# Experts on sorted slots of token-expert pairs with gathered weights, and mixed heads by the turning product

## The chip, the cores and the metric

The kernel runs on one core of a Trainium2 chip, all in f32. The metric is device time in microseconds of one execution. The engines are TensorE (PE; its weight loads are listed apart as PEld), VectorE (DVE), ScalarE (ACT), GpSimd (POOL) and SyncE (SP, which issues the DMAs). Each engine executes its own instructions in order; they wait for each other by semaphores.

## The reference

A pre-norm decoder of four layers, twelve sublayers in a row, each `x = x + f(layernorm(x))` on x of 8 x 256 x 256. Two of them are touched. Sublayer 3 is a mixture of 8 experts with 2 chosen for each token, and one shared expert that all tokens pass through (256 wide, 512 hidden):

```python
router_probs = softmax(flat @ router_w + router_b)          # flat: 2048 x 256
topk_probs, topk_idx = top_k(router_probs, 2)
weights = zeros_like(router_probs).at[arange(T)[:, None], topk_idx].add(topk_probs)
shared_out = gelu(flat @ sw1 + sb1) @ sw2 + sb2
h1 = gelu(einsum('td,edh->teh', flat, rw1) + rb1[None])
expert_out = einsum('teh,ehd->ted', h1, rw2) + rb2[None]
return shared_out + einsum('ted,te->td', expert_out, weights)
```

Sublayer 4 is attention with 16 heads of 16, whose scores are mixed over the heads before the softmax and whose probabilities are mixed over the heads behind it (q and k are turned by rope):

```python
dots = einsum('bhid,bhjd->bhij', q, k) * 16 ** -0.5
attn = softmax(einsum('bhij,gh->bgij', dots, w_pre))
attn = einsum('bhij,gh->bgij', attn, w_post)
out = einsum('bhij,bhjd->bhid', attn, v)
return out.transpose(0, 2, 1, 3).reshape(B, T, E) @ w_out.T + b_out
```

## The kernel before

x stays in SBUF for the whole kernel, as four blocks of 512 tokens (two sequences each), a block being four tiles of 128 tokens. Two threads of the program, left (blocks 0 and 1) and right (blocks 2 and 3), each go through the twelve layers: ssm, perceiver16, moe, talking, biased, routed, windowed, perceiver4, signs, recurrent, crossed, ternary. Each layer is a generator that yields after a small piece of work. `build` interleaves the two by a virtual time: the table `SHARE` says how long a layer is to last, `steps_of` how many pieces it has, and the right thread starts 1.01 x `SHARE[ssm]` later and runs so much faster that both end together. A scheduler in the framework then fixes each engine's order of instructions and the semaphores. So while one thread is in one layer, the other's work of an earlier or later layer fills the engines.

All of `Net`'s helpers are shared by both threads. `mms` (L361) issues the matmuls of a sum, so most matmuls have that line; `together` (L369) issues column-group matmuls, whose stationary operand is 32 or 64 columns wide, next to each other; `copy` takes PSUM to SBUF, two times of three on ACT (L353) and else on DVE (L355); `norm` computes a layer norm, its power on POOL (L382); `turned` transposes normed rows (L394); `add_rows` adds a bias to x on POOL (L421); `add_product` and `project` multiply by an output matrix and add to x on DVE (L428); `top2` ranks the router's probabilities by comparing each with each on DVE (L452 to L458).

`moe` (L760 on): per block a norm, its transpose `xt`, the router, softmax and `top2`; then a loop over the shared expert (-1) and the eight experts, each on all 512 tokens of each block: 4 x 2 matmuls of 512 columns (`mm<-xt,we`) with a gelu after each pair on ACT (L806), then for each of four tiles 4 matmuls of 256 columns (`o<-we,h`), whose result times the token's weight is added to x on DVE (L822). The weight is zero where the expert was not chosen. An expert's weights (1 MB) come by two DMAs of 512 KB on SP's queue (L795), two buffers of them.

`talking` (L846 on): per block a norm, q and k by `roped`, v; then for each sequence 16 steps, one for each output head h. A step scales q by column h of `w_pre` on DVE (`qs`, L875), so that the 256-wide product with k is already the mixed score; two tiles of 128 query tokens make 4 matmuls of 256 columns (`sc<-k,qs`), then a maximum (DVE L885), the exponential with its sum (ACT L889), the division (DVE L897, L899), four transposes (`pt`, L912), a copy (`pv`), and 4 matmuls of 256 columns against values that POOL has scaled by `w_post` for this head (`vh`, L903), summed in PSUM over all 16 steps (`o<-pv,vh`, L920).

The other layers that the prediction names: ssm (first; its rows reach SBUF by way of DRAM, the products on POOL are L593), perceiver16, `biased` and `routed` after `talking`, and a column-of-ones product in `ternary` (L1813).

Of the kernel before, what the change touches and what calls it, by code (L numbers as in the profile page):

```python
# [8 lines left out]
F32 = mybir.dt.float32  # L9
U8 = mybir.dt.uint8  # L10
AF = mybir.ActivationFunctionType
# [62 lines left out]
def constants():  # L74
# [21 lines left out]
    k.add("sums", (p[:, None] == 32 * np.arange(4)[None, :] + 16).astype(f))  # L96
    k.add("half", (p[:, None] // 64 == p[None, :] // 64).astype(f))
    for n in (8, 4):
        e = np.arange(n)
        k.add(f"before{n}", np.broadcast_to((e[None, :] < e[:, None]).astype(f).reshape(1, -1), (128, n * n)))  # L100
# [27 lines left out]
def layout(a):  # L128
# [37 lines left out]
    for k in ("ln_m_g", "ln_m_b", "ln_l_g", "ln_l_b"):  # L166
# [8 lines left out]
    p.add("rb1", a[n + "rb1"].reshape(8, 4, 128).transpose(2, 0, 1))  # L175
# [6 lines left out]
            a[n + "rw2"].reshape(8, 4, 128, 256).transpose(0, 2, 1, 3).reshape(8, 128, 1024),  # L182
        ],
        2,
    )
# [6 lines left out]
    p.mat("pre", np.repeat(a[n + "w_pre"].T, 16, axis=0))  # L192
    put("w3", p)
    rows("r3", ("post", a[n + "w_post"].T), ("bo", a[n + "b_out"]))
# [101 lines left out]
class Net:  # L296
# [145 lines left out]
    def top2(self, p, n, m, of=None):  # L442


        nc = self.nc
        rank = self.small.tile([128, n, m], F32, name="rank", tag=f"rank{m}")
        for i in range(n):
# [8 lines left out]
            nc.vector.tensor_reduce(rank[:, i, :], gt, AX.X, ALU.add)  # L456
        w = self.small.tile([128, n, m], F32, name="top", tag=f"top{m}")
        nc.vector.scalar_tensor_tensor(w, rank, 1.5, p if of is None else of, ALU.is_lt, ALU.mult)  # L458
# [43 lines left out]
def ssm(net):  # L502
# [3 lines left out]
    with net.scope(mm=2, y=1):  # L506
# [9 lines left out]
        for blk in net.blks:  # L516
# [19 lines left out]
            for d in "fb":  # L536
# [6 lines left out]
                nc.sync.dma_start(rows[d], dbc[d][64:96])  # L543
            yield
# [215 lines left out]
def moe(net):  # L760

    nc = net.nc
    with net.scope(mm=2, o=2):
        es = net.work
        w, r = net.weights(2)
        xts, tops = [], []
        for blk in net.blks:
            xt = net.normed_turned(blk, bufs=len(net.blks))
# [7 lines left out]
            p = net.small.tile([128, 4, 8], F32, name="probs", tag="probs")  # L776
# [7 lines left out]
            top = es.tile([128, 4, 8], F32, name=f"topall{blk}")  # L784
            nc.vector.tensor_copy(top, net.top2(p, 4, 8))
            tops.append(top)
            net.add_rows(blk, r["sb2"])
            yield
        for e in range(-1, 8):
            if e < 0:  # L790
                w1, w2, b1 = w["sw1"], w["sw2"], w["sb1"]
            else:
                we = es.tile([128, 2048], F32, name="we", bufs=2)
                for j in range(2):
                    nc.sync.dma_start(  # L795
                        we[:, j * 1024 : j * 1024 + 1024], net.d["experts"][e][:, j * 1024 : j * 1024 + 1024]
                    )
                w1 = we[:, :1024].rearrange("p (k m) -> p k m", k=2)
                w2 = we[:, 1024:].rearrange("p (k m) -> p k m", k=4)
                b1 = w["rb1"][:, e, :]  # L800
            for blk, xt, top in zip(net.blks, xts, tops):
                h = es.tile([128, 4, 512], F32, name="h", bufs=2)
                for c in range(4):
                    ps = net.bank()
                    net.mms(ps, [(w1[:, kc, c * 128 : c * 128 + 128], xt[:, kc, :]) for kc in range(2)])
                    nc.scalar.activation(h[:, c, :], ps, AF.Gelu, bias=b1[:, c : c + 1])  # L806
                    yield
                for i in range(4):
                    pairs = [(h[:, c, i * 128 : i * 128 + 128], w2[:, c, :]) for c in range(4)]
                    o = net.bank("o")  # L810
# [33 lines left out]


def talking(net):  # L846

    nc = net.nc
    with net.scope(mm=1, sc=1, pt=1, o=1):
        work = net.work  # L850
# [1057 lines left out]
```

## Time and profile before

| what | us |
|---|---|
| median of three runs (5421.10, 5433.18, 5438.67) | 5433.18 |
| profiled execution | 5411.81 |
| its span, first to last instruction | 5410.0 |
| mean granted TensorE clock in it | 0.91 |

In the profile, "x1024" behind a group counts instructions; the numbers behind the bar are busy time in us and mean ns of one; then the engine's idle time ahead of them and what ended it. An f32 matmul is two records of PE. PE's ends are modelled. The groups of the two layers, in numbers: the experts' first products 236.9 us and second ones 241.3 us of PE; the mixed heads' scores 293.6, transposes 94.1 and value products 265.0 us; the eight experts' DVE additions 61.8, `qs` 86.1, the maxima 88.1, ex times rc 99.6 us of DVE, `vh` 156.2 us of POOL. The left thread is in moe from about 1590 to 1950 us of the span and in talking until 2830; the right one in moe from 2450 to 2840 and in talking until 3510.

The DMA traffic of the whole span is 160 MB at a mean of 30 GB/s; all DMAs of before go out by SP.

### The profile page before, as it was taken

The numbers are of one execution on the slowest core, as the hardware profiler recorded it, in microseconds if no ns is written. First come the engines' busy times: TensorE is split into PE (matmuls) and PEld (weight loads), VectorE is DVE, ScalarE is ACT, GpSimd is POOL, SyncE is SP. The second block draws the span as 40 slices with busy tenths as digits, with TensorE's granted clock in tenths as the row PEclk, the third lists the DMA queues.
The fourth block names the chain that finished last, engine by engine and source line by source line (L and its number), as shares of the span: only waits on it lengthen the run. The fifth ranks groups of instructions, "written<-read, shape, count | busy, mean of one in ns | idle before, by whom it ended". The sixth has DMA issues, their size and how long they took to land.

```text
span 5410.0 us, 55906 instructions
## 1 busy us (share of the span) xinstructions
PE 4599.5 (85%) x20488; PEld 2846.3 (53%) x20488; DVE 2992.7 (55%) x5672; ACT 1981.2 (37%) x4524; POOL 1442.2 (27%) x1223
## 2 busy tenths in 40 slices
PE   5566567787889999999998899888898999988979
PEld 2121123343446556656766666655555677755656
DVE  6778788678781344442346554566556464243352
ACT  3444445445541433332432222323334332333221
POOL 3546534325340011110123422234121100232122
PEclk8888889898989999999999899986778999988989
DMA  3111121111110100001010000000001000010000
GB/s 97 48 47 55 50 82 49 32 31 45 41 60 24 57 14 1 1 7 36 24 35 1 34 1 1 29 13 34 12 1 41 8 6 32 1 51 35 2 32 16
DMA packets 95477, 160.15 MB, mean 30 GB/s; under 512 B 6651, under 2 KB 82275, under 8 KB 90851
## 3 DMA queue, kind: packets, MB, share of 16 engines
q1 hardware_dynamic: 95203, 156.58, 9.2%
q8 instruction: 162, 2.65, 0.2%
q14 instruction: 112, 0.92, 0.1%
HBM read 152.67 MB, written 3.88 MB: 29 GB/s over the span
## 4 chain that ended last, share of the span: by engine, by line
PE 51%; DVE 11%; ACT 4%; issue 3%; POOL 3%; POOLq 0%; ACTq 0%; DVEq 0%
PE mm L361 25%; PE o L361 6%; PE sc L369 5%; PE o L920 4%; PE sc L361 4%; PE av L369 3%; PE pt L912 1%; PE mm L705 1%; DVE xn L384 1%; ACT ex L889 1%; PE mm L394 1%; PE mm L1736 1%; DVE nm L885 1%; DVE ex L899 1%; DVE pv L355 1%
## 5 line engine op out<-in xcount | busy, mean ns | idle before, releaser
L609 PE MATMUL y<-hc,consts 128*128 128x512 f32 x1024 | 637.4, 724 | 334.7 <-DVE hc L603 333.3
L593 POOL TENSOR_TENSOR db<-du,rep 128x512 f32<-128x512 f32 x512 | 645.6, 1269 | 407.8 <-DVE mm L599 306.4
L599 DVE TENSOR_TENSOR_SCAN mm<-mm,db 128x512 f32<-128x512 f32 x512 | 619.0, 1220 | 62.3 <-ACT mm L585 62.0
L609 PEld LDWEIGHTS y<-hc,consts 128*128 128x128 f32 x1024 | 181.6, 211 | 669.7 <-DVE hc L603 630.8
L903 POOL TENSOR_TENSOR vh<-v,w 128x256 f32<-128x256 f32 x256 | 156.2, 631 | 955.2 <-PE o L920 927.3
L361 PE MATMUL mm<-xt,w 128*128 128x512 f32 (+1 forms) x896 | 359.5, 532 | 26.4 <-DVE rope_s L842 8.3
L603 DVE TENSOR_TENSOR hc<-mm,rep 128x512 f32<-128x512 f32 x512 | 348.2, 686 | 32.5 <-PE y L609 3.2
L585 ACT ACTIVATE mm<-dl,nega_b 128x256 f32<-128x256 f32 x512 | 241.0, 476 | 210.4 <-DVE hc L603 197.9
L585 ACT ACTIVATE mm<-dl,nega_f 128x256 f32<-128x256 f32 x512 | 239.9, 476 | 199.2 <-DVE hc L603 185.7
L361 PE MATMUL sc<-k,qs 128*128 128x256 f32 x1024 | 293.6, 404 | 22.2 <-ACT ex L889 21.3
L369 PE MATMUL sc<-k,q 64*128 64x333 f32 (+1 forms) x1152 | 260.1, 508 | 56.4 <-ACT pex L695 32.7
L353 ACT COPY pv<-mm 111x384 f32<-111x384 f32 (+2 forms) x334 | 172.5, 517 | 369.4 <-PE mm L705 178.8
L382 POOL TENSOR_TENSOR rs<-ve,neghalf 128x4 f32<-128x4 f32 (+1 forms) x57 | 58.9, 1034 | 887.3 <-DVE ve L380 806.5
L369 PE MATMUL av<-pv,v 111*64 111x256 f32 (+5 forms) x2752 | 254.0, 381 | 18.8 <-DVE pv L355 10.9
L920 PE MATMUL o<-pv,vh 128*128 128x256 f32 x1024 | 265.0, 395 | 5.2 <-ACT pv L353 3.5
L361 PE MATMUL mm<-h,sw 128*128 128x256 f32 x1024 | 242.5, 382 | 0.0
L361 PE MATMUL o<-we,h 128*128 128x256 f32 x1024 | 241.3, 380 | 1.0 <-DVE x L822 1.0
L361 PEld LDWEIGHTS mm<-xt,w 128*128 128x128 f32 x896 | 165.0, 197 | 146.7 <-issue 79.2
L705 PE MATMUL mm<-consts,pex 128*111 128x128 f32 x960 | 187.9, 308 | 63.5 <-DVE pex L701 32.9
L705 PEld LDWEIGHTS mm<-consts,pex 128*111 128x111 f32 x960 | 144.0, 191 | 185.3 <-DVE pex L701 52.0
L361 PE MATMUL mm<-xt,we 128*128 128x512 f32 x512 | 236.9, 594 | 0.3 <-ACT h L806 0.3
L361 PEld LDWEIGHTS sc<-k,qs 128*128 128x128 f32 x1024 | 187.5, 201 | 71.9 <-ACT ex L889 34.8
(372 smaller groups left out, 8512.2 us busy)
## 6 DMA issues: line engine op xcount, KB each, us to landing
we<-in_experts SPq DMA_DIRECT2D x32, 512.0 KB, 4.8
w<-in_w SPq DMA_DIRECT2D x12, 1024.0 KB, 6.9
w<-in_w SPq DMA_DIRECT2D x8, 1025.0 KB, 7.0
rep<-rows0f SPq DMA_DIRECT2D x32, 256.0 KB, 4.7
rep<-rows0b SPq DMA_DIRECT2D x32, 256.0 KB, 4.7
rep<-rows1f SPq DMA_DIRECT2D x32, 256.0 KB, 4.9
rep<-rows1b SPq DMA_DIRECT2D x32, 256.0 KB, 3.5
rep<-rows2f SPq DMA_DIRECT2D x32, 256.0 KB, 4.9
```

The source lines that it names most:

```text
L353: self.nc.scalar.copy(out, in_)
L361: self.nc.tensor.matmul(out, lhsT=lhs, rhs=rhs, start=n == 0, stop=n == len(pairs) - 1)
L369: self.nc.tensor.matmul(out, lhsT=lhs, rhs=rhs, start=start, stop=stop, tile_position=at)
L382: nc.gpsimd.tensor_tensor(rs[:rows], ve[:rows], self.neghalf[:rows, :n], ALU.pow)
L585: nc.scalar.activation(st[:, m * S : (m + 1) * S], dl[:, 2 * c + m, :], AF.Exp, scale=neg_a[d][:, 2 * c + m, n : n + 1],)
L593: nc.gpsimd.tensor_tensor(pairs_of(db), du[:, 2 * c : 2 * c + 2, :], bc[:, n % 2, 0, :].unsqueeze(1).to_broadcast(both), ALU.mult,)
L599: nc.vector.tensor_tensor_scan(st[:, order], st[:, order], db[:, order], 0.0, ALU.mult, ALU.add)
L603: nc.vector.tensor_tensor(pairs_of(hc), pairs_of(st), bc[:, n % 2, 1, :].unsqueeze(1).to_broadcast(both), ALU.mult,)
L609: nc.tensor.matmul(y[c], lhsT=net.ident, rhs=hc, start=d == "f" and n == 0, stop=d == "b" and n == 15,)
L705: nc.tensor.transpose(pt[:CH, j * 128 : j * 128 + 128], ex[:, e, j * CH : (j + 1) * CH], net.ident)
L903: nc.gpsimd.tensor_tensor(vh[:, j, :].rearrange("p (g e) -> p g e", g=H), v[:, 2 * b + j, :].rearrange("p (g e) -> p g e", g=H), r["post"] ...
L920: nc.tensor.matmul(o[:, c * S : (c + 1) * S], lhsT=vh[:, j, c * 128 : c * 128 + 128], rhs=pv[:, j, :], start=h == 0 and j == 0 and c == 0, ...
```

## The change

**Experts.** The tokens' ranks are kept (`ranks`, split off from `top2`). `places` counts, over the side's 8 tiles, how many pairs of token and chosen expert each expert has (a product with a lower triangle of ones and one with all ones, `ahead` and `ones`), lays the experts out in slots of 128 rows, and gives for each token the row of its two pairs (`rows`), their probabilities (`gate`), and for each slot the rows of its expert's weights in DRAM (`which`). There are 2 x 8 + 7 = 23 slots a side, enough for any choice. Each tile's normed rows are written by two indirect DMAs (POOL's queue) to the table `slots` in DRAM, which was filled with zeros by one DMA on SP in ssm. `read_after` makes the slots' loads wait for all 16 of these writes, and `apart_from_each_other` says that they don't overlap one another. The shared expert runs on all tokens as before. Then each slot: its expert's weights with the bias `rb1` (128 rows of 2052 values) by an indirect DMA on POOL's queue, three buffers; its rows from `slots` by SP; two transposes, a copy, 8 matmuls of 128 columns, 4 gelus, 4 matmuls of 256 columns, a copy, and a store to the table `results` by SP. At the end each token tile gets its two rows by two indirect DMAs from `results` and adds them with their probabilities.

**Mixed heads.** A step no longer is one output head but two groups of 8 tokens with all 16 heads: the stationary operand `qs` holds 16 heads x 8 tokens, made on POOL. Maximum, exponential and sum are the same. Instead of transposing ex, it is multiplied by `mix` (`blend`, which is `w_post` where the token is the same and zero elsewhere, times the reciprocal sums), which transposes and mixes the heads in one product ("turning product"). `pv` of all 16 steps is kept; v is kept in two copies with the odd or the even heads zeroed; at the end of a sequence 32 column-group matmuls make the output. PSUM has two banks for scores, none for `o`.

`SHARE` of moe goes from 270 to 150, and its `steps_of` with it. The diff's core, mostly its new lines (the removed ones are those of `moe` and `talking` above):

```diff
     k.add("sums", (p[:, None] == 32 * np.arange(4)[None, :] + 16).astype(f))
+    k.add("eighth", (p[:, None] % 8 == np.arange(8)[None, :]).astype(f))
     k.add("half", (p[:, None] // 64 == p[None, :] // 64).astype(f))
+    k.add("ahead", (p[:, None] < p[None, :]).astype(f))
+    k.add("row", p[:, None].astype(f))
+    k.add("slots", np.broadcast_to(np.arange(32, dtype=f)[None, :], (128, 32)))
+    k.add("slotrows", np.broadcast_to(np.arange(8, dtype=f)[None, :] * f(128), (128, 8)))
...
-    p.add("rb1", a[n + "rb1"].reshape(8, 4, 128).transpose(2, 0, 1))
...
+            a[n + "rb1"].reshape(8, 4, 128).transpose(0, 2, 1),
         ],
         2,
...
+    ).reshape(8 * 128, 2052)
...
+    p.add("post", np.repeat(a[n + "w_post"].T, 8, axis=0))
     put("w3", p)
-    rows("r3", ("post", a[n + "w_post"].T), ("bo", a[n + "b_out"]))
+    rows("r3", ("bo", a[n + "b_out"]))
...
+            if blk == net.blks[0]:
+                table = net.base.slots[net.side][0]
+                ns = table.shape[0] // 128
+                zero = work.tile([128, D], F32, name="zero")
+                nc.gpsimd.memset(zero, 0.0)
+                nc.sync.dma_start(
+                    table.rearrange("(s p) c -> p s c", p=128), zero.unsqueeze(1).to_broadcast([128, ns, D])
...
+    nt = 4 * len(net.blks)
+    ns = 2 * nt + 7
...
+        nc.vector.scalar_tensor_tensor(top, rank, 1.5, probs, ALU.is_lt, ALU.mult)
+        rows, gate, which = places(net, nt, ns, ones, rank, probs)
+        spread = []
+        for t in range(nt):
+            for k in range(2):
+                spread.append(
+                    nc.gpsimd.indirect_dma_start(
+                        table,
+                        bass.IndirectOffsetOnAxis(ap=rows[:, k, t : t + 1], axis=0),
+                        xns[t // 4][:, t % 4, :],
+                        None,
+                )
+        apart_from_each_other(net, spread)
+        yield
+        def shared(n):
...
+        for n in range(len(net.blks)):
+            yield from shared(n)
+        for s in range(ns):
+            we = es.tile([128, 2052], F32, name="we", bufs=3)
+            nc.gpsimd.indirect_dma_start(
+                we, None, net.d["experts"], bass.IndirectOffsetOnAxis(ap=which[:, s : s + 1], axis=0)
+            )
+            w1 = we[:, :1024].rearrange("p (k m) -> p k m", k=2)
+            w2 = we[:, 1024:2048].rearrange("p (k m) -> p k m", k=4)
+            xs = es.tile([128, D], F32, name="xs", bufs=3)
+            read_after(net, nc.sync.dma_start(xs, table[s * 128 : s * 128 + 128, :]), spread)
+            ps = net.bank()
+            for kc in range(2):
+                nc.tensor.transpose(ps[:, kc * 128 : kc * 128 + 128], xs[:, kc * 128 : kc * 128 + 128], net.ident)
+            xt = es.tile([128, 2, 128], F32, name="xst", bufs=2)
+            nc.vector.tensor_copy(xt, ps[:, :256].rearrange("p (k t) -> p k t", k=2))
+            ps = net.bank()
+            h = es.tile([128, 4, 128], F32, name="hs", bufs=2)
+            for c in range(4):
+                cols = slice(c * 128, c * 128 + 128)
+                net.mms(ps[:, cols], [(w1[:, kc, cols], xt[:, kc, :]) for kc in range(2)])
+            for c in range(4):
+                nc.scalar.activation(
+                    h[:, c, :], ps[:, c * 128 : c * 128 + 128], AF.Gelu, bias=we[:, 2048 + c : 2049 + c]
+                )
+            yield
+            o = net.bank("o")[:, :D]
+            net.mms(o, [(h[:, c, :], w2[:, c, :]) for c in range(4)])
+            ys = es.tile([128, D], F32, name="ys", bufs=2)
+            net.copy(ys, o)
+            nc.sync.dma_start(results[s * 128 : s * 128 + 128, :], ys)
+            yield
+        for t in range(nt):
+            xs = net.x(net.blks[t // 4], t % 4)
+            for k in range(2):
+                got = es.tile([128, D], F32, name="got", bufs=4)
+                nc.gpsimd.indirect_dma_start(
+                    got, None, results, bass.IndirectOffsetOnAxis(ap=rows[:, k, t : t + 1], axis=0)
+                )
+                nc.vector.scalar_tensor_tensor(xs, got, gate[:, k, t : t + 1], xs, ALU.mult, ALU.add)
+            yield
+def places(net, nt, ns, ones, rank, probs):
...
+    sel = es.tile([128, 2, nt, 8], F32, name="sel")
+    for n in range(2):
+        nc.vector.tensor_scalar(sel[:, n], rank, float(n), None, ALU.is_equal)
+    cum = es.tile([128, nt + 1, 8], F32, name="cum")
+    nc.vector.memset(cum[:, 0, :], 0.0)
+    for t in range(nt):
+        nc.vector.scalar_tensor_tensor(cum[:, t + 1, :], rank[:, t, :], 1.5, cum[:, t, :], ALU.is_lt, ALU.add)
+    mine = es.tile([128, nt, 8], F32, name="mine")
+    nc.vector.tensor_scalar(mine, rank, 1.5, None, ALU.is_lt)
+    ps = net.bank()
+    flat = lambda v: v.rearrange("p t e -> p (t e)")
+    net.mms(ps[:, : nt * 8], [(k["ahead"], flat(mine)), (ones, flat(cum[:, :nt, :]))])
+    net.mms(ps[:, nt * 8 : nt * 8 + 8], [(ones, cum[:, nt, :])])
...
+    gate = es.tile([128, 2, nt], F32, name="gate")
+    at = es.tile([128, 2, nt], F32, name="at")
+    rows = es.tile([128, 2, nt], I32, name="rows")
+    each = es.tile([128, 2, nt, 8], F32, name="each")
+    for out, v in ((at, pos), (gate, probs)):
+        nc.vector.tensor_tensor(each, sel, v.unsqueeze(1).to_broadcast([128, 2, nt, 8]), ALU.mult)
+        nc.vector.tensor_reduce(out, each, AX.X, ALU.add)
+    nc.vector.tensor_copy(rows, at)
...
+    expert = es.tile([128, ns], F32, name="expert")
+    nc.vector.tensor_reduce(expert, past, AX.X, ALU.add)
+    nc.vector.tensor_scalar(expert, expert, 7.0, 128.0, ALU.min, ALU.mult)
+    nc.vector.tensor_scalar(expert, expert, k["row"], None, ALU.add)
+    which = es.tile([128, ns], I32, name="which")
+    nc.vector.tensor_copy(which, expert)
+    return rows, gate, which
...
+def apart_from_each_other(net, writes):
+    key = f"spread_{net.side}"
+    for ins in writes:
+        net.tc.add_to_no_dep_group(key, ins.ins)
+        net.tc.declare_no_dep(ins.ins, group=key, reason="rows of their own")
+def read_after(net, read, writes):
+    for ins in writes:
+        net.tc.add_manual_dep(
+            read.ins,
+            ins.ins.name,
+            mybir.DependencyInfo(mybir.DependencyClass.Sync, mybir.DependencyReason.DATA),
+            reason="written by it",
...
+    with net.scope(mm=1, sc=2, pt=1):
...
+        nc.vector.tensor_scalar(w["pre"], w["pre"], 0.25, None, ALU.mult)
+        blend = work.tile([128, H, 8], F32, name="blend")
+        nc.vector.tensor_tensor(
+            blend,
+            w["post"].unsqueeze(2).to_broadcast([128, H, 8]),
+            net.k["eighth"].unsqueeze(1).to_broadcast([128, H, 8]),
+            ALU.mult,
+        )
+        blend = blend.rearrange("p h t -> p (h t)")
+        v = zeroed(net, [128, 4, 2, D], "v", 1)[0]
...
+            xt = net.normed_turned(blk, bufs=1)
...
+            q = work.tile([128, 2, 512], F32, name="q")
+            k = work.tile([128, 2, 512], F32, name="k")
...
+                for e in range(2):
+                    net.copy(one_parity(v[:, i, e, :], e), one_parity(ps, e))
...
+                pv = work.tile([128, 2, 32, 128], F32, name="pv")
+                for n in range(0, 32, 2):
+                    qs = work.tile([128, 2, 2, 128], F32, name="qs", bufs=2)
+                    wide = [128, 2, H, 8]
...
+                        t0 = b * S + 8 * n
+                        nc.gpsimd.tensor_tensor(
+                            qs[:, kc].rearrange("p n (h t) -> p n h t", h=H),
+                            q[:, kc, t0 : t0 + 16].rearrange("p (n t) -> p n t", n=2).unsqueeze(2).to_broadcast(wide),
+                            w["pre"][:, kc, :].unsqueeze(1).unsqueeze(3).to_broadcast(wide),
+                            ALU.mult,
...
+                        net.mms(sc[:, i * S : (i + 1) * S], [(qs[:, kc, i, :], k[:, kc, tok]) for kc in range(2)])
...
+                    for i in range(2):
...
+                    mix = work.tile([128, 2, 128], F32, name="mix", bufs=2)
...
+                        nc.vector.tensor_scalar(mix[:, i, :], blend, rc[:, i : i + 1], None, ALU.mult)
...
+                            net.mms(
+                                pt[:, j * S + i * 128 : j * S + i * 128 + 128],
+                                [(ex[:, i, j * 128 : j * 128 + 128], mix[:, i, :])],
...
+                    net.copy(pv[:, :, n : n + 2, :], pt.rearrange("p (j n m) -> p j n m", j=2, n=2))
+                    yield
+                av = net.bank()
+                group = []
+                for c in range(2):
+                    for e in range(2):
...
+                            for rr in range(4):
+                                rg, h = 32 * rr, 8 * c + 2 * rr + e
+                                group.append(
+                                    (
+                                        av[rg : rg + 32, c * S : (c + 1) * S].rearrange("p (n t) -> p n t", t=8),
+                                        v[:, 2 * b + j, e, 128 * c + rg : 128 * c + rg + 32],
+                                        pv[:, j, :, 8 * h : 8 * h + 8],
+                                        e == 0 and j == 0,
+                                        e == 1 and j == 1,
+                                        (0, rg),
+                                    )
+                                )
+                net.together(group)
...
+                net.copy(ao, pairs_of(av))
...
-SHARE = (620, 300, 270, 300, 80, 140, 140, 120, 170, 110, 160, 100)
+SHARE = (620, 300, 150, 300, 80, 140, 140, 120, 170, 110, 160, 100)
...
-        moe: 1 + 9 * 8,
+        moe: 1 + 0.5 + 8 + 23 + 4,
...
+        base.slots = {
+            side: [base.dram.tile([23 * 128, D], F32, name=f"{name}_{side}") for name in ("slots", "results")]
+            for side in ("left", "right")
+        }
```

The loop over the experts of before, and in it the two DMAs of 512 KB, are removed with it.

## Prediction

> **What bounds the kernel now.** I read the busy totals, then the busy time by stretches of the span, then the chain of waits inside the mixture of experts, then the costliest groups.
>
> ```profile
> PE 4599.5 (85%) x20488; PEld 2846.3 (53%) x20488; DVE 2992.7 (55%) x5672; ACT 1981.2 (37%) x4524; POOL 1442.2 (27%) x1223
> ```
> ```profile
> 1590.00:1950.00 360.00, 349.26 (x1318) 216.21 (x1316) 120.37 (x338) 120.08 (x203) 19.85 (x14) 0.99 0.13 45
> 1950.00:2450.00 500.00, 458.05 (x2158) 304.16 (x2156) 230.61 (x594) 175.11 (x528) 66.75 (x95) 0.97 0.02 8
> 2450.00:2840.00 390.00, 386.74 (x1616) 265.41 (x1616) 131.43 (x354) 139.47 (x236) 48.34 (x58) 1.00 0.08 26
> 2840.00:3510.00 670.00, 606.02 (x3336) 424.16 (x3337) 364.53 (x811) 192.16 (x557) 213.62 (x227) 0.94 0.03 13
> ```
> ```profile
> 1690.28 6.87 PE mm L361 x16
> 1697.15 6.91 PE o L361 x32
> ```
>
> The first line gives the average; the four stretches are where both touched layers run (left experts, left mixed heads, right experts, right mixed heads; columns: length, then busy time of PE, weight load, DVE, ACT, POOL, then granted clock, DMA share, GB/s). PE is busy 349+458+387+606 = 1800 of 1920 us, 94%, at clock 0.94 to 1.00: time taken from PE here shortens the span nearly one for one. The chain shows one expert on one block of 512 tokens: 6.87 + 6.91 = 13.78 us, with no gap. DMA is nearly idle.
>
> ```profile
> L361 PE MATMUL sc<-k,qs 128*128 128x256 f32 x1024 | 293.6, 404 | 22.2 <-ACT ex L889 21.3
> L920 PE MATMUL o<-pv,vh 128*128 128x256 f32 x1024 | 265.0, 395 | 5.2 <-ACT pv L353 3.5
> L912 PE MATMUL pt<-consts,ex 128*128 128x128 f32 x512 | 94.1, 290 | 14.9 <-DVE ex L899 14.1
> L369 PE MATMUL av<-pv,v 128*32 128x256 f32 x512 | 40.5, 441 | 2.4 <-ACT pv L1245 2.4
> L1813 PE MATMUL o<-ones,sq 128*128 128x1 f32 x256 | 33.2, 250 | 6.5 <-POOL sq L1810 6.4
> we<-in_experts SPq DMA_DIRECT2D x32, 512.0 KB, 4.8
> w<-in_w SPq DMA_DIRECT2D x8, 1025.0 KB, 7.0
> ```
>
> An f32 matmul is two records, a transpose one. From the chain a record costs 6.87/16 = 0.43 us at 512 columns, 6.91/32 = 0.216 at 256. Narrower ones meet the weight load: L1813's groups (one column) show 8 loads in 0.97 us, so 0.111 apart, and four L912 transposes take 0.51, 0.123 each.
>
> **Experts.** Removed: 8 experts x 4 blocks x 13.78 = 441 us of PE. The two router parts, the shared expert and the four norms stay. Added: 2 x 23 slots of 128 rows. A slot is 16 records at 128 columns (estimate 0.111 each from L1813: 1.78), 8 at 256 (1.73) and 2 transposes (0.25), 3.76 us; 46 x 3.76 = 173. The order of PE's instructions puts few other matmuls between a slot's halves, so a slot costs its own chain: the last of four gelus after the last first-half matmul (about 0.39, row L1381 for 128x128), then the last second-half matmul. I take 0.8 more, up to 4.5 us: +35 for 46.
>
> Each slot needs its expert's 1.05 MB, a gather issued by POOL, three buffers deep. The nearest rows are 1025 KB in 7.0 us for one load and, in the first 10 us, 276 GB/s at DMA share 0.85, so some 325 GB/s when full: 4.0 us a slot with loads overlapping, 7.0 without. I take 4.0, under the 4.5. Before, the expert loads were hidden behind 27 us of PE work per expert; now the cover is one slot. No gather or scatter is in this trace. One costs POOL between an SP issue (0.33 to 0.43 us) and its longest ordinary operation here (L421, 2.3 us); I take 1.3, near POOL's fixed cost in L382 (1.03), as the descriptors of 128 rows are its own work.
>
> New waits, per side. All 16 scatters must land before slot 0 may be read: places() is some 27 small DVE operations (0.2 us) plus 3 matmuls and their hops, 9 us; 16 x 1.3 = 21; landing and load 5: 35 us, and 19 us of shared-expert matmuls lie over it. But slot 0's transposes stand on PE ahead of the last four shared output tiles, so nothing of the other thread queued behind them runs either: 16 us, +32 for both. After the last slot: its store (2.9, as the 512 KB output stores land), 16 gathers (21; each addition, 0.48 on DVE, hides under the next gather), the last addition and the norm (7) make 31 us before the mixed heads' projections; left has about 10 us of the perceiver's matmuls queued there, right the routed layer's: 20 us open, +40. In POOL's queue the right gathers have routed's small operations (0.7 to 2.0 us, 16 of them) between them, and every x addition and norm root waits behind gathers; Each slot's two issues on SP (0.4 us each) and its DVE copy lie beside its 4.5 us. SP's queue holds the next layer's 4 MB of weights behind slot loads 0 to 3, which wait for scatters: those weights are needed tens of microseconds later and stay covered.
>
> One 3.0 MB zero fill per side enters SP's queue ahead of ssm's row loads: 3.0/325 = 9 us; the first is issued under the first loads at about 49 us of the span. Bounds 0 to 10, I take 5. Sum of experts: -441 + 173 + 35 + 32 + 40 + 5 = -156.
>
> **Mixed heads.** 128 steps stay 128 steps, with scores alike (8 records of 256). Removed: the value product, 8 records x 0.216 = 1.73 each, 221. The 4 transposes become 4 matmuls of 128 columns: 8 x 0.111 - 4 x 0.123 = +0.40, +51. Added: 32 column-group matmuls per sequence, the form and count of the L369 row above: +40. PE loses 130 us. Per step DVE loses qs (2 x 0.37) and swaps ex*rc (0.43) for a 128-wide product (0.3); POOL swaps vh (2 x 0.63) for qs in the same size, so about 1.3 us against 2.6 of PE: covered, though qs now heads the step's chain where vh stood at its end. The zero-padded v costs one POOL fill per side (128x2048, some 5 us at db's 1.27 per 512 columns), before v is needed. Two qs buffers and two score banks let it run a step ahead; if that cover failed, a hop and 1.3 us on 128 steps would be 170 us. PE was busy 458/500 and 606/670 there, so I book 85%: -110.
>
> Total -266: 5411.8 (profiled execution, span 5410.0) - 266 = 5146. The shown median, 5433.2, stands 0.4% over that execution, so the same change on it gives 5167; I forecast 5160.
>
> A rule that speaks against it, with its row first:
>
> ```profile
> 1603.59 2.34 POOL L421 TENSOR_TENSOR x<-x,w 128x1024 f32<-128x1024 f32 x1 [1.66 <-DVE xn L384]
> 1604.65 1.36 DVE L452 TENSOR_TENSOR gt<-probs 128x64 f32<-128x64 f32 x1
> ```
>
> A 0.21 us DVE comparison took 1.36 and ended with POOL's addition. The Trainium skill, "SBUF — State Buffer", describes an exclusive port pair shared by DVE and GpSimd, and warns that DMAs issued by GpSimd stall when DVE holds it, since the descriptors cannot be written. By that rule each of the 64 scatters and result gathers could lose one DVE operation (0.48 us, L822): an estimate of 31 us, 5190 in all, a part of rival 1's price. The row agrees that one of the two engines waits out the other, here DVE.
>
> On the other side, "DMA: Bandwidth & Descriptors" (Trainium skill, section on the anatomy of one DMA) fits a GpSimd DMA as 2 us plus its bytes at 436 GB/s: an estimate of 4.4 us for 1.05 MB, by which rival 2 falls away; the trace has no such DMA, and its own loads of that size took 7.0.
>
> **Rivals.**
> 1. *The waits eat the gain.* If POOL needs 2.3 us per scatter and gather (its L421 row) and the x loads trail, each side loses 16 x 1.0 twice more: 64; if the mixed heads also realise half (65, not 110), 45 more; the later layers, shifted against each other, 20. 5160 + 129 = 5290. For it: PE is in order and the threads' layers no longer meet as before; against it: the trace shows PE fed from the other thread in 94% of these stretches.
> 2. *Slots bound by the weight gather* (the slower side). 46 gathers of 1.05 MB: if they do not overlap, or run at half the rate of the 7.0 us row, a slot takes 13 us, not 4.5: 46 x 8.5 = +391, less 266 = +125, 5560. It decides from 266/46 = 5.8 us more, a slot above 10.3 us. For it: a load of this size takes 7.0 us from issue to landing, all gathers share POOL's queue behind other work, and nothing here shows one. Against: three buffers, and four 512 KB loads at once reached 325 GB/s in the first microseconds.
> 3. *All new waits hidden* by the other thread: the 72 us of waits and the 35 of slot chain shrink by 90: 5070. For it: left mixed heads now run beside the perceiver, right experts beside routed; against: the PE order above.
> 4. *The experts' layer does not do less work*, that is, the slots' padding fills it: 23 slots are fixed by the code, against 8 x 8 tiles, so this is excluded but for rival 2. A null result needs waits of just 266: 5433.
>
> **How the numbers follow.** Forecast 0.50; rival 1, 0.20; rival 3, 0.12; rival 2, 0.14; near no change, 0.04. Within 0.3% (16 us, what the three times' spread lets one tell) is "same": 0.04. Rival 2's share and a little of 1's tail are slower: 0.15; faster 0.81. Leaving out most of rival 2 above, and gains over 400, the range is 5030 to 5420. The likeliest one's own range: 130 us more waits or later-layer shifts of 40 either way, 5080 to 5290.
>
> **What would show it.** In the profile after: slot groups of matmuls of 128 columns at 0.11 to 0.13 us spacing and slots 4 to 5 us apart (if 7 or more, waiting for DMA we, rival 2); PE idle before slot 0's transposes, released by DMA, 10 to 20 us a side, and before the mixed heads' first projection 15 to 25; PE busy near 4200; the value product's 265 us gone and 40 to 45 of column groups instead; turning matmuls at 0.11 to 0.13. In the mixed heads PE's waits for POOL qs should stay under 20 us; more says the moved multiplication binds. Wrong at once if slots wait for weights, if scatters take over 2.5 us each, or if PE stays below 85% in the experts' stretch.

## The result and the profile after

| | us |
|---|---|
| before, median of 4 runs (5416.78 to 5438.67) | 5427.14 |
| after, median of 4 runs (5061.90 to 5068.83) | 5065.77 |
| ratio, 95% interval | 0.9333 [0.9311, 0.9356] |
| profiled execution of after: span, mean granted clock | 5063.3, 0.887 |

The changed kernel is 6.7% faster, 361 us. The forecast was 5160; 5066 lies inside its range, below its likeliest band and next to rival 3 (5070). The gain is 1.36 times the one that I summed.

First the totals of the page of after.

```profile
PE 4245.2 (84%) x20160; PEld 2651.3 (52%) x20160; DVE 2883.9 (57%) x5444; ACT 1897.9 (37%) x4574; POOL 1543.1 (30%) x1339
```

PE lost 4599.5 - 4245.2 = 354 us of busy time, and the span 347: PE's idle time is what it was, 811 before and 818 after. The waits that I added must have been paid back somewhere.

The stretches of after, in the columns that the prediction explained: left experts, left mixed heads up to the start of the right experts, right experts, right mixed heads.

```profile
1588.00:1795.00 207.00, 175.20 (x922) 133.15 (x920) 81.50 (x276) 65.17 (x167) 67.71 (x66) 0.92 0.57 198
1795.00:2450.00 655.00, 606.62 (x3462) 413.26 (x3461) 340.51 (x799) 252.27 (x743) 143.79 (x170) 0.96 0.02 7
2450.00:2650.00 200.00, 176.02 (x913) 136.49 (x915) 77.49 (x256) 48.13 (x137) 99.44 (x93) 0.85 0.57 198
2650.00:3105.00 455.00, 434.40 (x2744) 305.99 (x2741) 225.43 (x535) 168.25 (x523) 143.98 (x179) 0.97 0.02 9
```

The experts' stretches shrank from 360 and 390 to 207 and 200 us; they now have 24 to 32 us without PE each, where they had 3 to 11, and DMA moves 198 GB/s instead of 26 to 45. Right mixed heads took 670 us with 64 idle; now 455 with 21 idle. (The left ones' stretch, 655 us with 48 idle, is not the same work as the 500 with 42 before, as the right experts begin at another point of it.)

The groups of after that answer to those of before:

```profile
L369 PE MATMUL sc<-k,qs 128*128 128x256 f32 x1024 | 264.3, 386 | 1.5 <-ACT ex L1072 1.1 <-POOL k L1011 0.2
L369 PE MATMUL pt<-mix,ex 128*128 128x128 f32 x1024 | 150.7, 283 | 11.2 <-DVE mix L1083 6.7 <-DVE pv L363 2.0 <-DVE st L385 0.9
L377 PE MATMUL mm<-pv,v 128*32 128x256 f32 x512 | 29.3, 381 | 0.0
L369 PE MATMUL mm<-xst,we 128*128 128x128 f32 x736 | 90.5, 276 | 1.5 <-DMA we<-in_experts,which 1.5
L369 PE MATMUL o<-we,hs 128*128 128x256 f32 x368 | 90.2, 388 | 0.6 <-ACT hs L881 0.4
L872 PE MATMUL mm<-consts,xs 128*128 128x128 f32 x92 | 18.1, 280 | 10.3 <-DMA xs<-slots_left 5.3 <-DMA xs<-slots_right 5.0
L828 POOL DMA_INDIRECT slots_left<-xn,rows x16 | 15.6, 976 | 22.2 <-DVE expert L968 17.6 <-issue 4.3 <-DMA slots_left<-xn,rows 0.3
```

Read the idle part of each row: PE waited 1.5 us in all 46 slots for gathered weights, 0.6 us ahead of the slots' second products, 5.3 and 5.0 us for the first slot's rows, and for scores it hardly waits any more (1.5; before 22.2, of which 21.3 for the exponentials). That wait for the exponentials stands in a row of before which the prediction shows and does not use. The column groups (`mm<-pv,v`) take 29.3 us, the prediction took 40.

A slot, in the chain of waits of after (start, length, what):

```profile
1680.53 1.78 PE mm L369 x16
1682.53 0.86 PE mm L369 x2
1683.39 1.73 PE o L369 x8
1685.12 1.78 PE mm L369 x16
```

Slots are 4.59 us apart here; 0.86 of that is the other thread's matmuls, 0.22 the two transposes. A slot's own time is 1.78 + 0.22 + 1.73 = 3.73 us; the estimate was 3.76. The gelus are mostly hidden by the transposes and the other thread's matmuls, so the 0.8 for the chain was not paid.

### The profile page after: what moved, and what is told of

It reads as the page before. It is cut to its first block, busy times and chain, and to the rows that moved or that the text cites. A ratio compares the mean times of both kernels' runs of the same rounds, so it can differ in the third digit from the quotient of the medians.

```text
span 5063.3 us, 55466 instructions
## 1 busy us (share of the span) xinstructions
PE 4245.2 (84%) x20160; PEld 2651.3 (52%) x20160; DVE 2883.9 (57%) x5444; ACT 1897.9 (37%) x4574; POOL 1543.1 (30%) x1339
## 4 chain that ended last, share of the span: by engine, by line
PE 46%; DVE 11%; issue 4%; ACT 4%; POOL 3%; DMA 1%; POOLq 0%; DVEq 0%; ACTq 0%; SPq 0%
PE mm L369 23%; PE sc L377 6%; PE sc L369 4%; PE av L377 3%; PE o L369 3%; PE pt L369 2%; PE mm L726 1%; DVE xn L392 1%; PE mm L402 1%; PE mm L1918 1%; PE mm L1259 1%; PE mm L1579 1%; DVE hn_sq L1636 1%; ACT pv L361 1%; PE mm L377 1%
## 5 line engine op out<-in xcount | busy, mean ns | idle before, releaser
L1058 POOL TENSOR_TENSOR qs<-q,w 128x256 f32<-128x256 f32 x256 | 156.7, 633 | 472.8 <-PE sc L369 472.3
L377 PE MATMUL av<-pv,v 111*64 111x256 f32 (+5 forms) x2752 | 264.3, 397 | 12.2 <-ACT pv L361 6.3
L369 PE MATMUL sc<-k,qs 128*128 128x256 f32 x1024 | 264.3, 386 | 1.5 <-ACT ex L1072 1.1
L369 PE MATMUL mm<-kv,w 128*128 128x256 f32 (+1 forms) x640 | 209.6, 450 | 18.0 <-ACT q L766 10.0
L377 PEld LDWEIGHTS sc<-k,q 64*128 64x128 f32 (+1 forms) x1152 | 119.0, 210 | 191.3 <-ACT pex L716 58.1
L716 ACT ACTIVATE pex<-sc,pnm 128x333 f32<-128x333 f32 x320 | 169.8, 536 | 123.7 <-DVE pnm L712 121.8
L369 PE MATMUL mm<-w,ao 128*128 128x256 f32 x768 | 205.8, 409 | 7.0 <-DVE x L436 4.5
```

The costliest lines, as they stand in the source:

```text
L369: self.nc.tensor.matmul(out, lhsT=lhs, rhs=rhs, start=n == 0, stop=n == len(pairs) - 1)
L377: self.nc.tensor.matmul(out, lhsT=lhs, rhs=rhs, start=start, stop=stop, tile_position=at)
L716: nc.scalar.activation(ex[:, e, :], sc[:, e, :NK], AF.Exp, bias=nm[:, e : e + 1], accum_out=sm[:, e : e + 1])
L1058: nc.gpsimd.tensor_tensor(qs[:, kc].rearrange("p n (h t) -> p n h t", h=H), q[:, kc, t0 : t0 + 16].rearrange("p (n t) -> p n t", n=2).unsq ...
```

## Experiments

| run | median us | ratio to before, interval |
|---|---|---|
| after | 5065.77 | 0.9333 [0.9311, 0.9356] |
| e1 experts alone | 5244.68 | 0.9661 [0.9640, 0.9681] |
| e2 heads alone | 5238.83 | 0.9643 [0.9623, 0.9663] |
| e3 SHARE 270 | 5058.44 | 0.9312 [0.9295, 0.9329] |
| e4 two weight buffers | 5111.86 | 0.9416 [0.9397, 0.9435] |
| e5 heads alone, one bank | 5317.68 | 0.9791 [0.9775, 0.9808] |
| e6 no scatter wait | 5079.57 | 0.9340 [0.9320, 0.9360] |
| e7 no result gathers | 5012.41 | 0.9227 [0.9212, 0.9242] |
| e8 qs on VectorE | 5081.80 | 0.9357 [0.9341, 0.9372] |
| e9 four tiles late | 5060.18 | 0.9334 [0.9302, 0.9365] |
| e10 late, SHARE 270 | 5029.42 | 0.9266 [0.9240, 0.9293] |
| e11 late, 270, more buffers | 5046.20 | 0.9304 [0.9279, 0.9330] |
| e12 late, SHAREs 230 | 5056.06 | 0.9319 [0.9290, 0.9348] |

**e1 and e2, the two parts.** e1 is the changed kernel with the whole of `talking` and its weights' layout as before; e2 is the kernel before with the new `talking`. The first lines of the edits:

```diff
-    with net.scope(mm=1, sc=2, pt=1):
+    with net.scope(mm=1, sc=1, pt=1, o=1):
...
```

for e1, and for e2, against the changed kernel too (it also has the old `moe`),

```diff
-SHARE = (620, 300, 150, 300, 80, ...
+SHARE = (620, 300, 270, 300, 80, ...
...
-        moe: 1 + 0.5 + 8 + 23 + 4,
+        moe: 1 + 9 * 8,
...
```

> The experts' part of the change and its SHARE of 150 alone, the mixed heads as before. Theory A (the new waits were mis-sized in the prediction): by the profile after, 441 us of expert products go and 46 slots of 3.8 us come (175), with 10 us of waits for the scatters and 29 us of waits behind the last slots, so -441 + 214 = -227: 5200 us. Rival B (the prediction's own sum for this part was right, and the rest of the gain comes from the two parts together or from the mixed heads): -156, 5271 us.

> The mixed heads' part alone, experts and SHARE as before. Theory A: what is left of the measured -361 after the experts' -227 is -134, 5293 us, that is the whole PE time taken out (130) and no 85% of it. Rival B (prediction's term): -110, 5317 us. Rival C: the mixed heads are worth much more than their PE time because the step's chain got shorter (no sum over 16 steps in one PSUM bank, two score banks): -200, 5227 us.

The experts give 188 us and the heads 194, each against its own runs of before. The experts lie between theory A (5200) and rival B (5271); the heads come near rival C (5227), whose reason e5 tests. By ratios the parts sum to 0.0339 + 0.0357 = 0.0696 and together they give 0.0667: within the intervals they add up. So the 95 us missing from my sum are 32 in the experts and 84 in the heads, less 21 that the runs can't tell from zero.

**e3, SHARE of before.**

```diff
-SHARE = (620, 300, 150, 300, 80, ...
+SHARE = (620, 300, 270, 300, 80, ...
```

> The changed kernel with SHARE of the experts' layer back at 270, so that the two threads meet elsewhere. Theory A (the time comes from PE work taken out; where the threads meet matters little): within 25 us of 5066. Rival B (the missing 95 us of my sum came from the new meeting of the layers): 5066 plus 60 to 100 us, 5126 to 5166.

Theory A: 5058, no difference that the intervals show. The gain does not come from the new table of times.

**e5, the second bank.** The heads alone, with one score bank.

```diff
-    with net.scope(mm=1, sc=2, pt=1):
+    with net.scope(mm=1, sc=1, pt=1):
```

> The mixed heads' part alone (5239 us), but with one PSUM bank for the scores, as before the change, in place of two. Theory A (beside PE work the change takes out the wait of the next scores for the exponentials that still read the one bank: PE idle fell from 119 to 73 us in the stages up to the end of the mixed heads): 25 to 60 us of the 194 are lost again, 5264 to 5300. Rival B (the gain beyond PE work comes from the step's shorter chain, with no product of values in it): within 10 us of 5239.

79 us are lost again, more than theory A's 60; rival B is out. Without the bank the part is worth 118 us. PE busy is 4469.8 us in e2 and 4465.4 in e5, so the whole difference is waiting. The scores' rows of PE and its weight load, first e5, with one bank:

```profile
L363 PE MATMUL sc<-k,qs 128*128 128x256 f32 x1024 | 288.4, 402 | 39.8 <-ACT ex L906 28.9 <-POOL qs L892 4.5 <-issue 4.2
L363 PEld LDWEIGHTS sc<-k,qs 128*128 128x128 f32 x1024 | 184.7, 198 | 99.7 <-POOL qs L892 45.7 <-issue 30.8 <-ACT ex L906 3.8
```

and e2, with two:

```profile
L363 PE MATMUL sc<-k,qs 128*128 128x256 f32 x1024 | 272.8, 391 | 3.7 <-issue 3.1 <-POOL qs L892 0.3
L363 PEld LDWEIGHTS sc<-k,qs 128*128 128x128 f32 x1024 | 181.1, 194 | 46.0 <-issue 24.8 <-POOL qs L892 5.3 <-POOL q L845 0.2
```

With one bank PE waits 28.9 us for the exponentials, which still read the bank, and its weight load 45.7 for `qs` on POOL, which itself waits for PE to be done with the previous ones. With two, both waits all but vanish: PE's scores run a step ahead, and the moved `qs` is covered. The kernel before, with one bank and `qs` on DVE, had 21.3 us for the exponentials in PE's row, and in its weight load's row:

```profile
L361 PEld LDWEIGHTS sc<-k,qs 128*128 128x128 f32 x1024 | 187.5, 201 | 71.9 <-ACT ex L889 34.8
```

So the new step with one bank waits more than the old one did.

The same stretch, from the end of ssm to the right mixed heads' last exponentials, before:

```profile
1590.00:3506.00 1916.00, 1796.56 (x8390) 1207.50 (x8388) 845.07 (x2085) 623.94 (x1511) 347.19 (x392) 0.97 0.06 20
```

in e5 and e2 (one bank, two banks),

```profile
1590.00:3395.00 1805.00, 1652.55 (x8334) 1106.30 (x8335) 758.39 (x1827) 602.62 (x1501) 345.84 (x392) 0.97 0.06 21
1590.00:3294.00 1704.00, 1630.78 (x8257) 1096.29 (x8255) 759.15 (x1835) 578.73 (x1466) 349.23 (x393) 0.97 0.07 23
```

and in e1:

```profile
1590.00:3322.00 1732.00, 1557.29 (x8120) 1097.98 (x8120) 819.27 (x2116) 560.82 (x1580) 453.07 (x503) 0.95 0.15 52
```

Length less PE busy is PE's idle time: 119 before, 152 with the new heads on one bank, 73 on two, 175 with the new experts. (The other thread stands a little elsewhere at the end of each stretch, so these are not exact.) Of the bank's 79 us, then, 33 are waits that the new step would have added, and 46 are waits that the kernel before already had. The heads take these 46 us of idle out, the experts put 55 in, and so it came that the changed kernel has hardly more idle than before.

**e4, two buffers of weights.**

```diff
-            we = es.tile([128, 2052], F32, name="we", bufs=3)
+            we = es.tile([128, 2052], F32, name="we", bufs=2)
```

> Two buffers of gathered weights in place of three. A slot is 4.2 us apart, a gather lands 6.8 us after its issue. Theory A (the gathers are hidden only by being three deep): with two, a slot's period is half of landing (6.8) + first products (1.9) + gelu and second products (2.4), 5.6 us, so 46 x 1.4 = +64; if the landing shortens to its least, 5.6 us, 5.0 and +35: 5101 to 5130 us. Rival B (gathers far from binding): at most +10, 5076. If it goes above +180, the gathers come one at a time and rival 2 of the prediction was close.

+46 us, theory A. The slots' first products in e4:

```profile
L369 PE MATMUL mm<-xst,we 128*128 128x128 f32 x736 | 96.8, 285 | 35.8 <-DMA we<-in_experts,which 32.5 <-DVE m_Wk L1333 1.3 <-DVE prc L720 1.0
```

32.5 us of waits for weights, 1.5 with three buffers. The gathers land 6.8 us (median) after their issue in after and 6.0 in e4, a slot is 4.2 to 4.6 us, and it is the third buffer that hides the difference. Rival 2 (+391 us) was far off even with two buffers.

**e6, no wait for the scatters.**

```diff
+            side: [... for name in ("slots", "results", "blank")]
...
-            read_after(net, nc.sync.dma_start(xs, table[s * 128 : s * 128 + 128, :]), spread)
+            nc.sync.dma_start(xs, blank[s * 128 : s * 128 + 128, :])
```

> The changed kernel, with the slots' rows loaded from a third table, filled with zeros in ssm like the other was, and never written afterwards; so no load waits for the scatters, which still run. The experts then work on zero rows: the output is not the reference's. Theory A (the wait is what the profile after shows, 5.3 + 5.0 us of PE): 5050 to 5060 us from 5066. Rival B (the prediction's 16 a side): 5034. Rival C (slots begin only when the gathered weights are there, which are issued behind the scatters): no change, within 5 us.

Rival C as to the time: no gain (0.9340 against 0.9333). Left slot 0's transposes in after, on PE's timeline:

```profile
1645.01 0.66 PE L872 MATMUL mm<-consts,xs 128*128 128x128 f32 x2 [5.28 <-DMA xs<-slots_left]
```

and what stands ahead of them in e6:

```profile
1645.06 1.98 PE L369 MATMUL mm<-xt,w 128*128 128x512 f32 x4 [2.53 <-ACT h L844]
1649.93 3.68 PE L369 MATMUL mm<-xt,w 128*128 128x512 f32 x4 [2.88 <-ACT h L844]
1653.67 0.38 PE L872 MATMUL mm<-consts,xs 128*128 128x128 f32 x2
```

The 5.3 us wait is gone, and the shared expert's products wait 2.5 + 2.9 us for gelus just before. On the right side it is partly as rival C said: PE waits 6.8 us for gathered weights there, 1.5 in after. Why ACT was late on the left in e6 and not in after, I did not settle. The two profiles are also no exact pair: in e6 the first layer norm's power on POOL comes 6.1 us later (1594.29 against 1588.17), well ahead of the first slot's load. From there slot 0's transposes start 59.4 us later in e6 and 56.8 in after, so the missing wait did not bring them forward.

**e7, no gathers of results.**

```diff
-        for t in range(nt):
-            xs = net.x(net.blks[t // 4], t % 4)
-            for k in range(2):
-                got = es.tile([128, D], F32, name="got", bufs=4)
...
```

> The changed kernel without the 32 gathers of results and their additions to x; the routed experts' part is left out of the output. Theory A (PE stands idle about 18 us behind the left slots and 11 behind the right ones): 5037 to 5048 us. Rival B (prediction, 20 us a side): 5026. Rival C (the next layer's norm is late anyway): within 8 us of 5066.

-53 us, more than any theory. In after, PE's own waits in the left experts' stretch (what waited, for what: total, times, longest):

```profile
PE mm L726 <- DVE pex L722: 10.8, 2, 7.8
PE sc L377 <- ACT pex L716: 5.4, 1, 5.4
PE mm L872 <- DMA xs<-slots_left: 5.3, 1, 5.3
```

The first two, 16 us, lie behind the last slot, where only the perceiver's softmax chain of the other thread was left to run: the wait is put down to ACT and DVE, but PE stands idle because the left thread has nothing for it until its gathers are in. In the 31 us from 1764 on PE is busy 12.1 us in after and 26.2 in e7. The left side's last second products and the mixed heads' first projection, in after,

```profile
1761.59 1.99 PE L369 MATMUL o<-we,hs 128*128 128x256 f32 x8 [0.45 <-ACT hs L881]
1796.85 1.98 PE L369 MATMUL mm<-xt,w 128*128 128x512 f32 x4
```

and in e7:

```profile
1769.06 1.99 PE L369 MATMUL o<-we,hs 128*128 128x256 f32 x8 [0.44 <-ACT hs L881]
1778.01 1.88 PE L369 MATMUL mm<-xt,w 128*128 128x512 f32 x4
```

That is 35.3 us in after and 9.0 in e7. On the right side it is 35.3 (2616.10 to 2651.44) and 8.6 (2651.55 to 2660.11). So the gathers and their additions hold up the threads by 26 and 27 us, 53 in all. That a thread's delay comes through in full is not shown: PE itself was idle for about 19 and 11 us of the two tails, the right thread of e7 stands only 10 us ahead at its last exponential of the mixed heads (3091.0 against 3101.1), and the 53 are only complete at the end.

**e8, qs on VectorE.**

```diff
-                        nc.gpsimd.tensor_tensor(
+                        nc.vector.tensor_tensor(
                             qs[:, kc].rearrange("p n (h t) -> p n h t", h=H),
```

> The changed kernel with the products qs on VectorE in place of GpSimd. Theory A (the move to GpSimd is free since GpSimd is idle in the steps, and VectorE has its 0.69 + 0.16 + 0.64 us a step already): 256 more operations of 0.4 to 0.6 us, 100 to 150 us on VectorE, of which 10 to 40 come through: 5076 to 5106. Rival B (the port shared by the two engines costs more than the move saves): faster by 10 or more, under 5056.

+16 us by medians, theory A, but the intervals overlap. The 256 products take 101.5 us of VectorE, and at most a sixth of it comes through. The move to GpSimd did no harm that can be seen.

**e9 to e12, towards a faster kernel.** The last four tiles of the shared expert behind the slots; e10 to e12 add to that what their expectations say.

```diff
-        for n in range(len(net.blks)):
-            yield from shared(n)
+        late = shared(len(net.blks) - 1)
+        for n in range(len(net.blks) - 1):
+            yield from shared(n)
+        for _ in range(4):
+            yield next(late)
...
+        yield from late
         for t in range(nt):
```

On top of it, e10 (first line), e11 (e10 and the next two) and e12 (the last instead of the first):

```diff
+SHARE = (620, 300, 270, 300, 80, ...
+            we = es.tile([128, 2052], F32, name="we", bufs=4)
+                got = es.tile([128, D], F32, name="got", bufs=8)
+SHARE = (620, 300, 230, 230, 80, ...
```

> The changed kernel, with the last four output tiles of the shared expert (10.6 us of PE a side) moved behind the last slot, ahead of the gathers of results. In the changed kernel they stand behind slot 0's transposes, where they cover only slot 0's way to its first products. Theory A (leaving the gathers out took 54 us, so the tail behind the last slot is what costs; work put there hides it): 10 to 20 us faster, 5046 to 5056. Rival B (what is moved is missed at slot 0 as much): within 8 us of 5066.

> The same four late tiles with SHARE of the experts back at 270. Theory A (the two edits are independent, -15 and -7): 5040 to 5050 us. Rival B (with 270 the other thread's work already fills the tail): like SHARE 270 alone, 5054 to 5062.

> The same as the run before, with four buffers of weights in place of three and eight of gathered results in place of four. Theory A (three weight buffers just cover the gathers, two cost 46 us; POOL waited 4 us for result buffers): 0 to 8 us faster than the run before. Rival B (more gathers in flight lengthen each, nothing gained): within 3 us.

> The four late tiles with SHARE 230 for the experts and 230 for the mixed heads (270 and 300 in the run of late tiles and 270), which became shorter too. Theory A (where the threads meet matters little): within 15 us of that run. Rival B (the stage behind the mixed heads takes 811 to 863 us according to how the threads meet, and that shows in the total): 20 us or more away from it, either way.

e9 gained nothing that can be told (rival B). e10, at 5029 us, is faster than both kernels and than either of its theories: its interval lies clear of the changed kernel's, 36 us by medians. But neither of its two edits gave a difference that could be told from zero alone, and with more buffers (e11, 5046) or other shares (e12, 5056: rival B by the medians) half or more of it is gone again, at overlapping intervals. I take it as a favourable meeting of the threads, not as a mechanism; that is not shown. More buffers did not help; e11 fits neither theory.

## Why the prediction was right, and where it was not

**Right: the bound.** PE sets the time in these stages, and most of its work was counted well. Turning matmuls run 8 in 0.89 us, 0.111 each; a slot's own time is 3.73 us against 3.76; in e2 PE's busy time fell by 4599.5 - 4469.8 = 130 us, the sum for the mixed heads.

**The step that failed: the mixed heads' -110, measured -194.** The prediction wrote "PE was busy 458/500 and 606/670 there, so I book 85%" (the shares are 92 and 90%; the 85 is worked out from nothing), and took the two score banks merely as cover for the moved `qs`. The old step had one bank, so each set of scores waited for the exponentials of the one before; the rows showed it (21.3 us of PE waits for ACT, 42 and 64 us idle). In the profiled executions the part is worth 5410.0 - 5234.8 = 175 us: the 130 of PE work in full and 46 of idle that went with the second bank. (The medians' 194 is larger, mostly because the profiled execution of before was a fast one, 5411.8 against the median of 5432.8 that e2 was held against.) A stage with 8 to 10% idle was read as one that gives back only part of a saving, when the change also removed a reason for the idleness. That the heads without the bank (e5) come to 118 us, near the 110, is luck: there the PE work is all saved, but the new step's waits for its single bank take a part of it away again.

**The experts' -156, measured -188.** In the profiled executions it is 5410.0 - 5243.5 = 166 us: PE's busy time fell by 235 and its idle time rose by 69. The prediction had 268 of PE work less 112 of waits and issue, so its sum, -156, lies so near because both of its sides were too large. Term by term: slots 173 predicted, 46 x 3.73 = 172 shown; chain of gelus 35, nothing shown (0.6 us of PE's idle time); scatter waits 32, 10 in the profile and nothing gained in e6; result waits 40, about 30 of PE idle in the two tails, 53 in e7; zero fills 5, too little to be told (the layer's first left power comes at 1588.17 in after, at 1593.30 before, at 1594.29 in e6). By -441 + 172 PE should have lost 269 us of busy time; 34 of these are missing, and I can't place them. The granted clock in the stretch to the right mixed heads' end was 0.95 in e1 and 0.97 before; whether this is where the 34 went, no run shows. The price of a slot's gather was also worked out wrongly, with nothing hanging on it: 1.05 MB at 325 GB/s is 3.2 us, not 4.0, and those 325 are themselves an estimate from 276 at a DMA share of 0.85.

**The signs.** Slots stand 4.2 to 4.6 us apart, PE is busy 4245 us, the scores' weight loads wait 4.7 us for `qs`, a scatter holds POOL 0.96 us: all as named. PE's idle time before slot 0 was smaller than named (5, not 10 to 20). One sign of being wrong came true: PE is busy 175.2 of 207 us in the left experts' stretch, just under 85%, mostly for the tail behind the last slot, and the time stayed inside the range all the same.

**Indirect DMAs.** I took 1.3 us of POOL each, unseen in the trace of before. The timeline of POOL in after:

```profile
1619.49 0.96 POOL L828 DMA_INDIRECT slots_left<-xn,rows  x1 [0.30 <-issue]
1620.76 0.96 POOL L828 DMA_INDIRECT slots_left<-xn,rows  x1 [0.30 <-issue]
```

0.96 us and a gap of 0.30, 1.26 apart. The rule of the Trainium skill, "SBUF — State Buffer" (section on its two separate sides), that VectorE can block descriptor writing, would have added an estimated 31 us. The longest of the 110 indirect DMAs held POOL 1.47 us, against a median near 0.95, and the sixteen left scatters sum to 15.6: the traces show nothing of that size, though VectorE was busy only 3.1 of the 27 us of the left scatters, so this is no hard test. The fit of the Trainium skill, "DMA: Bandwidth & Descriptors" (anatomy of one DMA), gave an estimated 4.4 us for a gather of 1.05 MB; here they landed 5.6 to 12.2 us after issue, 6.8 in the middle, with up to three in flight, so the measured time stands.

**Rivals.** Rival 3 named nearly the right time (5070), by luck: the new waits were not all hidden (e7), others went. Rival 2 fell with 1.5 us of waits for weights, rival 1 with the gain itself. The 94% that rival 1 gives for PE fed from the other thread is PE's busy share, whichever thread fed it.

**Given back later.** Behind the right mixed heads, up to the last exponentials of the windowed layer, before:

```profile
3506.00:4317.00 811.00, 715.58 (x4334) 458.69 (x4333) 468.83 (x983) 274.72 (x826) 199.78 (x136) 0.83 0.05 17
```

and after:

```profile
3101.00:3964.00 863.00, 766.81 (x4425) 488.82 (x4417) 474.95 (x970) 282.09 (x834) 199.01 (x136) 0.78 0.05 16
```

By 3101 the changed kernel was 405 us ahead; this stretch takes 52 us of it back, nearly all of it as more PE busy time at a lower granted clock (0.78, not 0.83). With SHARE 270 it takes 823 us at 0.82, but what lies ahead of it is 44 us longer, and the total is the same. I did not find what makes the clock lower there; that it depends on how the threads meet fits these three profiles and is not more than that.

## What to carry to other kernels

Before booking only a part of a saving because a stage has idle time, ask what ends that idle time and whether the change also removes it: here a second PSUM bank, freed by the way, took out 46 us of idle beside 130 of work, and kept the new step from adding 33. Experts on sorted slots pay in PE work (235 us of PE's busy time in e1, of 269 counted); of the waits that they add, the dearest found is not that for the gathers of weights, which three buffers hid, but the tail, where a thread has nothing for PE until its results are gathered back (53 us when left out). A wait that the profile shows may be worth nothing when it goes (e6): others came in its place.

## Not expected of the hardware

An indirect DMA of 128 rows holds POOL 0.94 to 0.96 us whether a row is 1 KB (`slots`, `got`) or 8 KB (`we`); only its landing differs, 2.4 and 2.8 against 6.8 us in the middle. All DMA together, gathered weights for the most part, moved 249 to 275 GB/s in the slots' stretches while PE ran at a granted clock of 0.98 to 1.00.
